# Windowed attention, second pass: where the probabilities of a group's last unit are added up

## The chip, the cores and the metric

The kernel runs on one core of one Trainium2 chip. The core has TensorE (PE in the profile, with PEld for its weight loads), VectorE (DVE), ScalarE (ACT), GpSimd (POOL) and SyncE (SP), which here only issues DMAs. The metric is the device time of one execution, in microseconds (us). Lower is better. Before the change it is 1713.32 us, the median of three runs.

## The reference, cut to what matters

The program is two transformer-like layers over 2048 tokens of width 512. The first is linear attention plus a mixture of experts, the second is windowed softmax attention plus a block over 256 chosen tokens. Everything is float32. Only the softmax attention of the second layer is touched. It has 16 heads of width 32, it is causal, and the window reaches back 1024 tokens:

```python
scores = jnp.einsum('bhqd,bhkd->bhqk', q, k) / np.sqrt(HD)
scores = jnp.where(mask[None, None, :, :], scores, NEG)   # 0 <= q_idx - k_idx <= 1024
attn = jax.nn.softmax(scores, axis=-1)
out = jnp.einsum('bhqk,bhkd->bhqd', attn, v)
out = out.transpose(0, 2, 1, 3).reshape(b, n, H)
return jnp.einsum('bnh,hm->bnm', out, w_out)
```

What the change is about is the denominator of that softmax: for each head and each query, the sum over the keys of exp(score - maximum).

## The kernel before, in words

A first pass over the scores, spread over earlier stages, finds every query's maximum. The second pass, which is the last stage of the program (from about 1342 us to the end at 1713.8 us), computes the scores again, takes the exponentials and does everything else.

The second pass goes over **groups** `(Q, g)`: Q is one of four blocks of 512 queries (four tiles of 128), g one of four sets of four heads. Their order is written out by hand in `order`: first (2,0), (0,0), (2,1), (0,1), (2,2), (0,2), (2,3), (0,3), then (1,0) to (1,3), then (3,0) to (3,3).

A group is a list of **units**, made by `units(Q)`. A unit is a block of 128 keys against the query tiles that can see it, or two blocks of keys that between them cover the four query tiles once. Blocks Q = 2 and Q = 3 have nine units, n = 0 to 8, each with all 512 queries. Q = 1 has eight units and Q = 0 has four, and there the last three are narrower: 384, 256 and 128 queries.

For one unit:

- `probabilities` has PE compute the scores into two PSUM tiles `ps` (L1296), take off the maxima (L1311) and add the masks (L1319). Then ACT takes the exponential (L1330) into two SBUF tiles of 128 keys x 2 heads x 512 queries. For n = 0 these tiles are the accumulators `acc0` and `acc1` (a pool of two per name), for the other units they are `pt` tiles (a pool of eight, so four units).
- `values` multiplies the probabilities with the values into the PSUM tile `av` (L1370).
- `gathered` adds the unit to the accumulators: `acc += pt`, two instructions of 128x1024 (L1403), on GpSimd for odd n and on VectorE for even n. For some units `summed(n)` returns True, and then `sums` is called for them instead.
- `sums` is a product of PE with a matrix of ones, `ones_f`: it sums over the 128 keys and puts the result into the PSUM tile `sm` (L1384). One such product is eight matmul instructions, two for each of the four heads. The first two heads read the first tile, the last two heads the second.

The program is software-pipelined by one unit: in the loop over the units PE first gets the scores of the next unit, then `values` and `gathered` of the unit before (`pending`).

When a group is through, its `ending` runs beside the units of the next group, one step for each unit:

```python
            for _ in range(3):
                yield
            self.sums(self.acc, 0, QT * P, True)
            for j in range(QT):
                js = slice(j * P, (j + 1) * P)
                V.reciprocal(self.sm[:, js], self.sm[:, js])
                V.tensor_tensor(aT[:, g, js], aT[:, g, js], self.sm[:, js], ALU.mult)
                if j % 2:
                    yield
```

So the product over the finished accumulators is issued with the next group's unit n = 3, just behind `values` and `gathered` of its n = 2. Four pairs of reciprocal and multiplication on VectorE follow (L1413, L1414). After the last head group, g = 3, four products with `w_out` (L1340) and four additions (L1344) give the output rows. Every engine takes its instructions in this order of the program.

Of the kernel before, what the change touches and what calls it, by code (L numbers as in the profile page):

```python
# [21 lines left out]
NT = T // P  # L22
D = 512
NC = D // P
# [14 lines left out]
def two_layer_kernel(ctx: ExitStack, tc: tile.TileContext, a: dict, out: bass.AP):  # L39
# [1227 lines left out]
    QT = 4  # L1267
# [79 lines left out]
    class Group:  # L1347
# [7 lines left out]
        def summed(self, n):  # L1355


            if (self.Q, self.g) == (NT // QT - 1, NC - 1) and n == len(self.us) - 2:
                return True
            return self.Q > 1 and n == len(self.us) - 1  # L1360

        def values(self, n, got):
            Q, g, unit = self.Q, self.g, self.us[n]
# [140 lines left out]
```

## Time and profile before

| | |
|---|---|
| median of three runs | 1713.32 us (1712.89 to 1716.47) |
| the profiled execution, its own time | 1715.47 us |
| its span, first to last instruction | 1713.8 us |
| mean granted TensorE clock | 0.994 |
| busy over the span: PE, DVE, ACT, POOL | 97%, 57%, 34%, 29% |
| busy from 1342 to 1480 us (Q = 2 and 0): PE, DVE, POOL | 137.86, 92.97, 108.28 of 138 us |
| busy from 1622 to 1695 us (most of (3,1) to (3,3)): PE, DVE, POOL | 73.00, 48.28, 58.87 of 73 us |
| products with `ones_f` (L1384) | 200 instructions, 25 products: 16 over accumulators, 9 over a single unit |

Busy time is read with care: the ends of matmuls are modelled, and a VectorE or GpSimd instruction counts as busy from its start to its end whether it works or is held up. A timeline row may merge instructions that follow one another; it then shows the form of the first, the time from the first start to the last end, and how many there are.

### The profile page before, as it was taken

Reading aid. Unit: us, or ns where it says so; the run is one execution under the profiler, and the core shown is the slowest. Engines: PE = TensorE matmul, PEld = TensorE weight load, DVE = VectorE, ACT = ScalarE, POOL = GpSimd, SP = SyncE. Lnnn points to the kernel's source line nnn. Section 1 sums busy time; section 2 is a strip of 40 time slices with the busy share of each in tenths; the row PEclk is TensorE's granted clock in tenths of the full one; section 3 lists DMA queues with packets and bytes.
Section 4 is the critical chain, followed back from the end, with each engine's and each line's share of the span. In section 5 each row is a group of like instructions: output and inputs, shape, how many; then the busy total and the mean of one; then the engine's idle time right before and its main releaser. Section 6 shows DMA issues by size and latency. Waiting matters only on the chain.

```text
span 1713.8 us, 20410 instructions
## 1 busy us (share of the span) xinstructions
PE 1657.4 (97%) x8114; PEld 743.6 (43%) x8114; DVE 982.5 (57%) x1256; ACT 588.2 (34%) x939; POOL 500.0 (29%) x398
## 2 busy tenths in 40 slices
PE   8999999999999999989999989899999999999999
PEld 3445444444444444444443434454564333333343
DVE  4754746345445543357566676675555477557565
ACT  3213333243253344221111110431100566447473
POOL 3230000000000200053574423330000677558584
PEclk9999999999999999999999999999899999999999
DMA  9411001120030431111010034112232300110101
GB/s 360 169 37 47 25 25 37 47 88 25 25 111 25 94 104 50 62 56 56 25 32 26 28 118 153 62 50 74 74 99 74 99 1 2 50 50 2 50 1 38
DMA packets 62384, 109.23 MB, mean 64 GB/s; under 512 B 12528, under 2 KB 14064, under 8 KB 61520
## 3 DMA queue, kind: packets, MB, share of 16 engines
q1 hardware_dynamic: 55856, 106.12, 18.7%
q0 software_dynamic: 1152, 1.21, 0.4%
q10 hardware_dynamic: 5280, 0.59, 0.3%
q8 instruction: 63, 1.03, 0.3%
q14 instruction: 33, 0.27, 0.1%
HBM read 86.24 MB, written 21.67 MB: 63 GB/s over the span
## 4 chain that ended last, share of the span: by engine, by line
PE 81%; DVE 10%; ACT 2%; DMA 2%; POOL 2%; issue 2%; SPq 0%; DVEq 0%; POOLq 0%; ACTq 0%
PE ea L494 6%; PE acc L478 6%; PE eg L492 6%; PE ps L1296 6%; PE pa L633 6%; PE p L965 6%; PE av L1370 5%; PE po L553 3%; PE pq L367 3%; PE po L1340 3%; PE gx L242 3%; DVE mx L645 3%; PE mg L1210 2%; PE pao L1175 2%; PE pm L1225 2%; PE po L555 2%
## 5 line engine op out<-in xcount | busy, mean ns | idle before, releaser
L645 DVE TENSOR_REDUCE mx<-pa 128x4 f32<-128x1536 f32 (+3 forms) x144 | 252.9, 1756 | 151.2 <-PE pa L641 72.2
L1403 POOL TENSOR_TENSOR acc<-acc,pt 128x1024 f32<-128x1024 f32 (+2 forms) x110 | 252.9, 2328 | 96.6 <-DVE acc L1403 43.4
L1330 ACT ACTIVATE pt<-ps 128x1024 f32<-128x1024 f32 (+3 forms) x208 | 181.4, 924 | 108.1 <-PE ps L1319 61.5
L1403 DVE TENSOR_TENSOR acc<-acc,pt 128x1024 f32<-128x1024 f32 (+1 forms) x80 | 144.4, 1832 | 103.9 <-POOL acc L1403 103.9
L633 PE MATMUL pa<-kT,qT 32*128 32x384 f32 (+3 forms) x1152 | 139.8, 541 | 19.8 <-DVE mx L645 16.1
L350 ACT ACTIVATE r_e<-eg 128x512 f32<-128x512 f32 x128 | 75.9, 594 | 201.6 <-PE eg L492 194.4
L1296 PE MATMUL ps<-qT,kT 32*128 32x512 f32 (+3 forms) x1152 | 139.9, 524 | 0.0
L352 DVE TENSOR_TENSOR h<-ea,r_e 128x512 f32<-128x512 f32 x128 | 87.2, 685 | 84.5 <-ACT r_e L351 83.5
L743 POOL TENSOR_TENSOR cosg<-cosg,gam 128x512 f32<-128x512 f32 x2 | 2.5, 1264 | 442.7 <-DVE gam L740 442.7
L492 PE MATMUL eg<-xl,rwgT 128*128 128x512 f32 x256 | 130.7, 592 | 0.0
L494 PE MATMUL ea<-xw,rw1T 128*128 128x512 f32 x256 | 130.7, 592 | 0.0
L478 PE MATMUL acc<-h,rw2T 128*128 128x512 f32 x256 | 129.2, 592 | 0.0
L965 PE MATMUL p<-w_qk,xnt 128*128 128x512 f32 x256 | 123.2, 604 | 2.3 <-DVE qk L758 2.3
L1370 PE MATMUL av<-pt,v 128*32 128x512 f32 (+3 forms) x1024 | 100.8, 482 | 0.0
L1296 PEld LDWEIGHTS ps<-qT,kT 32*128 32x128 f32 x1152 | 54.7, 183 | 94.7 <-issue 65.8
L633 PEld LDWEIGHTS pa<-kT,qT 32*128 32x128 f32 x1152 | 46.8, 185 | 103.3 <-DVE mx L645 64.9
L488 DVE TENSOR_TENSOR xw<-xw,xl 128x512 f32<-128x512 f32 x64 | 43.8, 685 | 83.5 <-DMA xw<-w_d 83.2
L351 ACT ACTIVATE r_e<-r_e 128x512 f32<-128x512 f32 x128 | 80.3, 629 | 5.7 <-ACT r_e L350 1.9
L478 PEld LDWEIGHTS acc<-h,rw2T 128*128 128x128 f32 x256 | 48.6, 190 | 61.3 <-issue 52.1
L492 PEld LDWEIGHTS eg<-xl,rwgT 128*128 128x128 f32 x256 | 48.6, 190 | 61.2 <-issue 61.0
L494 PEld LDWEIGHTS ea<-xw,rw1T 128*128 128x128 f32 x256 | 48.6, 190 | 61.2 <-issue 59.3
L288 PE MATMUL pk<-k_wT,xnT 128*128 128x512 f32 x128 | 61.3, 622 | 3.5 <-ACT xnT L117 3.5
(336 smaller groups left out, 2420.0 us busy)
## 6 DMA issues: line engine op xcount, KB each, us to landing
xw<-w_d SPq DMA_DIRECT2D x64, 256.0 KB, 3.2
x<-in_x SPq DMA_DIRECT2D x16, 256.0 KB, 4.7
res_d<-x SPq DMA_DIRECT2D x16, 256.0 KB, 2.1
xr<-res_d SPq DMA_DIRECT2D x16, 256.0 KB, 4.2
xn_d<-xn SPq DMA_DIRECT2D x16, 256.0 KB, 3.0
res_d<-xr SPq DMA_DIRECT2D x16, 256.0 KB, 3.1
xnq<-xn_d SPq DMA_DIRECT2D x16, 256.0 KB, 2.8
v_d<-vt SPq DMA_DIRECT2D x16, 256.0 KB, 2.0
```

The source lines that it names most:

```text
L351: S.activation(r, r, AF.Square)
L352: V.tensor_tensor(dst, pa, r, ALU.mult)
L478: PE.matmul(acc, rw2T[:, j, e, :], h, start=e == 0 and j == 0, stop=e == E - 1 and j == 1,)
L492: PE.matmul(pg, rwgT[:, e, hb], xl, start=True, stop=True)
L494: PE.matmul(pa, rw1T[:, e, hb], xw, start=True, stop=True)
L633: PE.matmul(pS[:, h, : w * P], qT[r, g, i * P : (i + 1) * P], kT[r, g, ks], start=True, stop=not (edge or last),)
L645: V.tensor_reduce(mx[:, g, :, c], pS[:, :, : w * P], AX.X, ALU.max)
L965: PE.matmul(pj, xnt[:, c, :], w, start=c == 0, stop=c == NC - 1)
L1296: PE.matmul(pS[h // 2][:, h % 2, t0 * P - q0 : (t1 + 1) * P - q0], kT[r, g, kb * P : (kb + 1) * P], qT[r, g, t0 * P : (t1 + 1) * P], start ...
L1330: S.activation(pT[:, :, :n], pS[hp][:, :, :n], AF.Exp)
L1370: PE.matmul(self.av[h * HD : (h + 1) * HD, t0 * P - o : (t1 + 1) * P - o], vs[kb // 4][:, kb % 4, hs], got[h // 2][:, h % 2, t0 * P - q0 : ...
L1403: eng.tensor_tensor(part, part, got[hp][:, :, : q1 - q0], ALU.add)
```

## The change

`summed` says which units are summed by a product of their own. Before, these were the last unit (n = 8) of every group with Q > 1, and also the last but one (n = 7) of the very last group (3,3). Now only the last two units of (3,3) are. The last units of (2,0) to (2,3) and (3,0) to (3,2), seven in all, are added to the accumulators by `gathered` as the others are. All have n = 8, so the code gives them to VectorE.

```diff
         def summed(self, n):
 
 
-            if (self.Q, self.g) == (NT // QT - 1, NC - 1) and n == len(self.us) - 2:
-                return True
-            return self.Q > 1 and n == len(self.us) - 1
+            return (self.Q, self.g) == (NT // QT - 1, NC - 1) and n >= len(self.us) - 2
```

In the instruction streams this takes 56 matmul instructions (7 products of 8) off PE, with their weight loads, and puts 14 additions of 128x1024 on VectorE, each pair between the pair for n = 6 and the next group's pair for n = 2. The `sm` tile of those groups is now first written by the product over the accumulators. The orders on GpSimd, ScalarE and SyncE stay as they were.

## The prediction

> **What bounds the kernel now.** I read the page first: its chain that ended last, then its costliest groups.
>
> ```profile
> span 1713.8 us, 20410 instructions
> ...
> PE 81%; DVE 10%; ACT 2%; DMA 2%; POOL 2%; issue 2%; SPq 0%; DVEq 0%; POOLq 0%; ACTq 0%
> ...
> L1403 POOL TENSOR_TENSOR acc<-acc,pt 128x1024 f32<-128x1024 f32 (+2 forms) x110 | 252.9, 2328 | 96.6 <-DVE acc L1403 43.4
> ...
> L1403 DVE TENSOR_TENSOR acc<-acc,pt 128x1024 f32<-128x1024 f32 (+1 forms) x80 | 144.4, 1832 | 103.9 <-POOL acc L1403 103.9
> ```
>
> PE carries the chain, so work off PE looks like gain. But both engines that add spend much of their time waiting for each other. So next I asked line 1403 for itself, with its min/median/max in ns, and the timelines of the two engines at the end of group (2,1):
>
> ```profile
> L1403 POOL TENSOR_TENSOR acc<-acc,pt x110: 720/2363/3406, 1342.8 to 1689.9; 128x1024 f32<-128x1024 f32 x78, 128x768 f32<-128x768 f32 x16, 128x256 f32<-128x256 f32 x16
> ...
> L1403 DVE TENSOR_TENSOR acc<-acc,pt x80: 677/1215/3386, 1345.8 to 1693.2; 128x1024 f32<-128x1024 f32 x64, 128x512 f32<-128x512 f32 x16
> ```
>
> ```profile
> 1392.22 4.50 DVE L1403 TENSOR_TENSOR acc<-acc,pt 128x1024 f32<-128x1024 f32 x2 [2.25 <-POOL acc L1403]
> ```
>
> ```profile
> 1388.78 5.72 POOL L1403 TENSOR_TENSOR acc<-acc,pt 128x1024 f32<-128x1024 f32 x2 [1.56 <-DVE acc L1403]
> ```
>
> ```profile
> 1395.72 9.11 POOL L1403 TENSOR_TENSOR acc<-acc,pt 128x1024 f32<-128x1024 f32 x4 [1.23 <-DVE acc L1403]
> ```
>
> VectorE's pair for n = 6 takes 4.50 us, though an addition of 1024 takes 1.21 alone. It starts at 1392.22, POOL's pair for n = 5 ends at 1388.78 + 5.72 = 1394.50, and VectorE ends at 1396.72: 2.22 after POOL, 1.1 for each addition. So an addition on VectorE does nothing while one on GpSimd runs. The two share something, here called the port, and the additions form one serial chain. The Trainium skill ("SBUF — State Buffer", "SBUF: two separate sides") names it: GpSimd and a VectorE instruction with two SBUF inputs exclude each other for a whole instruction. That speaks against this change; who goes next when both wait, it does not say, so by it alone the sum stays open between the first two rivals below.
>
> The last row holds four additions: n = 7 of (2,1), 5.56 us to 1401.28 (the row of a window that ends at 1400), then at once n = 1 of (0,1), narrower, 3.55 for both. Now the chain of waits at the same place:
>
> ```profile
> 1397.66 0.86 PE sm L1384 x8
> ...
> 1403.56 0.57 PE av L1370 x8
> 1404.13 0.86 PE sm L1384 x8
> 1404.98 1.07 PE ps L1296 x8
> ```
>
> One product costs PE 0.86 us. The first row is one that goes; the second is the product over the accumulators, which today finds them ready since 1401.28. Last, the tail:
>
> ```profile
> 1642.49 10.19 POOL L1403 TENSOR_TENSOR acc<-acc,pt 128x1024 f32<-128x1024 f32 x4 [1.22 <-DVE acc L1403]
> 1653.92 5.54 POOL L1403 TENSOR_TENSOR acc<-acc,pt 128x1024 f32<-128x1024 f32 x2 [1.23 <-DVE acc L1403]
> ```
>
> ```profile
> 1689.93 4.50 DVE L1403 TENSOR_TENSOR acc<-acc,pt 128x1024 f32<-128x1024 f32 x2 [2.26 <-POOL acc L1403]
> ```
>
> ```profile
> 1694.53 1.19 PE L1384 MATMUL sm<-acc,ones_f 128*32 128x512 f32 x8
> ```
>
> From n = 1 of (3,1) at 1622.54 to 1692.22 GpSimd never idles but for VectorE's turns of 1.22 to 1.56. VectorE's last pair ends at 1694.43 and the last product starts at 1694.53; the view of line 1384 puts 0.3 us of PE idle down to it. In the tail this serial chain, not PE, is already the bound, by a hair.
>
> **The change, part by part.** *Removed:* 7 products x 0.86 = 6.0 us of PE. GpSimd's and ScalarE's orders stay; `pt` buffers are held longer, at no cost: the tightest, those of n = 8 in (2,0), are wanted again by ACT at 1374.42 and will be free by 1372.4 (below).
>
> *Added:* 14 additions on VectorE, 2.22 us of port for each pair, behind GpSimd's pair for n = 7. Behind them in VectorE's queue stand the next group's n = 2 additions and the reciprocals; PE waits for them at the product over the accumulators, with all later scores behind it.
>
> *Who gets the port?* When GpSimd ends n = 7, VectorE waits for n = 8, and GpSimd has n = 1 of the next group queued (its row starts it without a gap). No L1403 row shows such a meeting. The nearest is elsewhere, in the timelines at 762 us, where both VectorE additions of steps and base read two SBUF tiles:
>
> ```profile
> 762.75 0.16 DVE L850 TENSOR_TENSOR thr_h<-steps,base_h 128x1 f32<-128x1 f32 x1
> 762.83 2.33 DVE L850 TENSOR_TENSOR thr_l<-steps,base_l 128x1 f32<-128x1 f32 x1
> ```
>
> ```profile
> 762.79 2.35 POOL L763 TENSOR_TENSOR t<-qk,cosg 128x1024 f32<-128x1024 f32 x1 [8.29 <-DVE base_h L860]
> 765.10 2.51 POOL L768 TENSOR_TENSOR t<-qk,sing 128x512 f32<-128x512 f32 x2
> ```
>
> GpSimd came between two back-to-back VectorE instructions, and thr_l then ended at 765.16, before GpSimd's next was through: they take turns, in the order in which they ask. I take **turns**: first half of n = 8, GpSimd's first half of n = 1 (3.55 / 2 = 1.78), second half of n = 8. One tiny instruction is thin evidence, so the ends stay: VectorE keeps the port for both halves, or GpSimd keeps it until its queue waits.
>
> *Groups (2,g), turns.* In (2,1) PE would come to the product at 1404.13 - 0.86 = 1403.27. The second half of n = 8 is done at 1401.28 + 1.1 + 1.78 + 1.1 = 1405.26. Then follow a handover of about 0.1 (1694.43 to 1694.53 above) and half to all of a product (0.43 to 0.86), so 0.5 to 0.95, say 0.7: PE goes on at 1405.96, not 1404.98, a loss of 1.0 net of the 0.86 gained. (2,2) and (2,3) have the same spacing. In (2,0) n = 7 ends at 1368.35 and PE goes on at 1370.55 (same views), so 1368.35 + 3.98 + 0.7 = 1373.03, a loss of 2.5. Sum 3 x 1.0 + 2.5 = +5.5 (4.6 to 6.4). Nothing later in these groups gives it back: GpSimd's n = 1 of the next one waits for PE.
>
> *Group (3,0):* GpSimd idles 11.66 us before 1622.54, so n = 8 is hidden and 0.86 is gained.
>
> *Tail:* the chain must take two more pairs, after (3,1) and (3,2): 2 x 2.22 = 4.4, or 3.9, since a GpSimd addition that had to wait is some 0.13 shorter afterwards (1401.28 - 1396.72 = 4.56 for a pair, against 4.69 for the pair at 1622.54, which did not wait) and with turns two more have to wait; I take +4.2. PE's own 2 x 0.86 there buys nothing, as PE is not last.
>
> Sum: 5.5 - 0.9 + 4.2 = **+8.8 us** (7.6 to 9.9). The profiled execution's 1715.47 (span 1713.8 and 1.67 around it) would become 1724.3; on the median of 1713.32, 2.15 lower, it is 1722.1. The measurement can tell a change of about 0.2%, 3.4 us.
>
> **The rivals.**
>
> *VectorE keeps the port.* Then n = 8 of (2,1) is done at 1401.28 + 2.22 = 1403.50 and PE goes on at 1404.2: 0.8 gained in each of three groups, 0.7 lost in (2,0), sum -1.7 (-2.0 to -0.6); with -0.9 and +4.3, +1.7 (1.0 to 2.9): 1715.0. For it: back-to-back VectorE instructions start up to 0.1 before the one ahead ends. Against it: the 762 rows.
>
> *GpSimd keeps the port.* n = 8 done at 1401.28 + 3.55 + 2.22 = 1407.05, PE at 1407.75: 2.8 lost three times and 4.3 once, 12.6. In the tail n = 8 waits for two full additions (4.65), PE stalls in (3,2) and again in (3,3), and ends some 5.2 later. Sum 12.6 - 0.9 + 5.2 = +16.9 (16 to 18): 1730.2. For it: GpSimd's rows follow each other without a gap. Against: thr_l got in.
>
> *All hidden (faster).* If a VectorE addition beside a GpSimd one took its 1.21 us, n = 8 of (2,1) would be done before 1403.27, and the chain of the tail would not grow: -6.0, 1707.3. The change decides for this side once a pair for n = 8 ends under 2.0 us after n = 7 and GpSimd's next pair is not put off. Against: 3386 ns, the longest of line 1403, and the 4.50 rows.
>
> The skill's "Perfetto Trace Analysis" ("Identifying the Most-Contended Engine") would judge by occupancy and relieve the busiest engine. By it, with PE at 97% and DVE at 57%, the change pays all that it takes off PE. The port's rows, which no occupancy shows, say otherwise and decide here.
>
> That the edit does less than it says can be excluded: the streams hold 56 matmuls fewer and 14 VectorE additions more.
>
> **How the numbers follow.** Turns 0.55, VectorE keeps 0.22, GpSimd keeps 0.13, hidden 0.10. Slower by over 0.2% are the first and third, 0.68; within 0.2% the second, 0.22; faster 0.10. The range runs from VectorE's low end, 1714.0, to 1729.5, the lower part of GpSimd's; left out are the rest of that and the hidden case. The likeliest case alone: 1720.9 to 1723.2.
>
> **What would show it.** Right: VectorE's pair for n = 8 of the (2,g) groups with an addition of GpSimd between its halves, PE idle for about 2 us for VectorE at the product over the accumulators in (2,1), 3 to 4 in (2,0), and the time from n = 1 of (3,1) to the last product longer by about 4. Wrong: n = 8 back to back (second case), or after both of GpSimd's (third), or products that wait for nothing.

## The result, and the profile after

| | before | after |
|---|---|---|
| median of five runs | 1713.32 us | 1722.46 us (1720.67 to 1722.95) |
| ratio | | 1.0049, 95% interval 1.0038 to 1.006 |
| profiled execution, span | 1715.47, 1713.8 us | 1720.67, 1719.0 us |
| first exponential of the second pass | 1337.96 us | 1334.08 us |
| from there to the end of the span | 375.81 us | 384.89 us |

The kernel became slower by 9.1 us, 0.5%. The two spans differ by 5.2 us only, because the stages ahead of the second pass, which nobody touched, took 3.9 us less in the profiled execution of after. So from here on all profiles are compared from the first exponential of the second pass (the first ScalarE row of line 1330 into `acc`) to the end. There the difference is 384.89 - 375.81 = 9.08 us, the same as that of the medians.

The page of after: the chain that ended last, and the two groups of additions, now line 1401.

```profile
span 1719.0 us, 20334 instructions
...
PE 75%; DVE 12%; POOL 4%; issue 3%; DMA 3%; ACT 3%; SPq 0%; DVEq 0%; POOLq 0%; ACTq 0%
...
L1401 POOL TENSOR_TENSOR acc<-acc,pt 128x1024 f32<-128x1024 f32 (+2 forms) x110 | 264.3, 2431 | 94.5 <-DVE acc L1401 40.9
L1401 DVE TENSOR_TENSOR acc<-acc,pt 128x1024 f32<-128x1024 f32 (+1 forms) x94 | 184.1, 1993 | 78.5 <-POOL acc L1401 76.5
```

PE has 56 matmuls less, and its share of the chain has fallen from 81% to 75%: the chain now runs through VectorE, GpSimd and "issue" instead. GpSimd has the same 110 additions as before, but they take 11.4 us longer: an addition that is held up counts as busy. Who waits for them is said by the view of the product's line (now 1382), before a row of 0.3 us, once:

```profile
  DVE acc L1401: 21.8, 16
```

This row adds the idle time of PE's weight loads to that of its matmuls, and the two overlap. The view of line 1401 has them apart; the matmuls alone wait six times, for 6.8 us:

```profile
  PEld sm L1382: 15.0, 10
  PE sm L1382: 6.8, 6
```

The timelines of VectorE and GpSimd at the end of (2,1), each for a window that ends before the next pair, and the chain of waits at the same place:

```profile
1397.68 6.12 DVE L1401 TENSOR_TENSOR acc<-acc,pt 128x1024 f32<-128x1024 f32 x2 [2.26 <-POOL acc L1401]
```

```profile
1397.60 5.12 POOL L1401 TENSOR_TENSOR acc<-acc,pt 128x1024 f32<-128x1024 f32 x2
```

```profile
1399.83 0.02 issue
1399.85 0.02 ACT pt L1330
1399.88 0.47 issue
1400.35 0.60 ACT pt L1330
1400.95 0.02 issue
1400.97 2.85 DVE acc L1401
1403.81 0.04 issue
1403.86 1.05 PE sm L1382 x4
1404.91 1.07 PE ps L1296 x8
```

VectorE's pair for n = 8 takes 6.12 us. The GpSimd row holds the second half of n = 7 (2.36 us, to 1399.96) and the first half of (0,1)'s n = 1, which ends at 1402.72. VectorE's first half ends at 1401.04, its second at 1403.80. So after n = 7 the order is VectorE, GpSimd, VectorE: turns, one addition each. PE's timeline shows what it does meanwhile:

```profile
1401.92 1.03 PE L1382 MATMUL sm<-acc,ones_f 128*32 128x512 f32 x4
1403.86 1.05 PE L1382 MATMUL sm<-acc,ones_f 128*32 128x512 f32 x4 [0.91 <-DVE acc L1401]
1404.84 1.14 PE L1296 MATMUL ps<-qT,kT 32*128 32x512 f32 x8
```

The first half of the product, four matmuls over the first accumulator, runs ahead. Then PE has no work that it may do for 0.91 us, until VectorE's second half is through. The other half of the product takes 1.05 us in the chain before the next scores.

The tail, on GpSimd's timeline, where the rows of four additions hold n = 7 of one group and n = 1 of the next:

```profile
1624.10 4.68 POOL L1401 TENSOR_TENSOR acc<-acc,pt 128x1024 f32<-128x1024 f32 x2 [10.95 <-PE av L1368]
...
1644.04 12.13 POOL L1401 TENSOR_TENSOR acc<-acc,pt 128x1024 f32<-128x1024 f32 x4 [1.23 <-ACT pt L1330]
...
1671.43 12.12 POOL L1401 TENSOR_TENSOR acc<-acc,pt 128x1024 f32<-128x1024 f32 x4 [1.23 <-ACT acc L1330]
```

The first of these rows of four took 10.19 us before and takes 12.13, the second 10.21 and 12.12: VectorE's two halves of n = 8 are inside them. The product over the accumulators of (3,2) now waits as well, as PE's timeline says:

```profile
1681.40 1.05 PE L1382 MATMUL sm<-acc,ones_f 128*32 128x512 f32 x4 [1.97 <-DVE acc L1401]
```

### The profile page after: what moved, and what is told of

It is laid out like the page before. It is cut to its first block, busy times and chain, and to the rows that moved or that the text cites. A ratio compares the mean times of both kernels' runs of the same rounds, so it can differ in the third digit from the quotient of the medians.

```text
span 1719.0 us, 20334 instructions
## 1 busy us (share of the span) xinstructions
PE 1657.5 (96%) x8058; PEld 742.3 (43%) x8058; DVE 1021.7 (59%) x1270; ACT 588.2 (34%) x939; POOL 511.5 (30%) x398
## 3 DMA queue, kind: packets, MB, share of 16 engines
q0 software_dynamic: 1152, 1.21, 0.4%
## 4 chain that ended last, share of the span: by engine, by line
PE 75%; DVE 12%; POOL 4%; issue 3%; DMA 3%; ACT 3%; SPq 0%; DVEq 0%; POOLq 0%; ACTq 0%
PE eg L492 6%; PE acc L478 6%; PE ea L494 6%; PE pa L633 6%; PE p L965 5%; PE ps L1296 4%; PE av L1368 4%; PE po L553 3%; PE pq L367 3%; PE po L1340 3%; PE gx L242 3%; DVE acc L1401 2%; DVE mx L645 2%; POOL acc L1401 2%; PE mg L1210 2%
## 5 line engine op out<-in xcount | busy, mean ns | idle before, releaser
L1401 POOL TENSOR_TENSOR acc<-acc,pt 128x1024 f32<-128x1024 f32 (+2 forms) x110 | 264.3, 2431 | 94.5 <-DVE acc L1401 40.9
L1401 DVE TENSOR_TENSOR acc<-acc,pt 128x1024 f32<-128x1024 f32 (+1 forms) x94 | 184.1, 1993 | 78.5 <-POOL acc L1401 76.5
L763 POOL TENSOR_TENSOR t<-qk,cosg 128x1024 f32<-128x1024 f32 x15 | 35.3, 2351 | 98.7 <-DVE qk L758 63.1
```

What stands on the lines that cost most here:

```text
L1401: eng.tensor_tensor(part, part, got[hp][:, :, : q1 - q0], ALU.add)
```

## Experiments

The theory tested is that of the prediction: an addition on VectorE and one on GpSimd exclude each other and take turns, which costs PE a wait in the groups of block 2 and lengthens a serial chain at the end. Its first rival is that VectorE simply has too much to do, the second that the whole loss lies in the tail. Ratios are to the kernel before on the same chip; the last column is the profile's, from the first exponential of the second pass to the end, against 375.81 us.

| kernel | median us | ratio, 95% interval | profile, us |
|---|---|---|---|
| changed kernel | 1722.46 | 1.0049 (1.0038 to 1.006) | +9.1 |
| change for block 2 alone | 1721.66 | 1.0042 (1.0028 to 1.0056) | +6.4 |
| change for block 3 alone | 1717.64 | 1.0019 (1.001 to 1.0028) | +2.9 |
| change for (3,0) alone | 1713.86 | 1.0 (0.9991 to 1.0009) | -0.8 |
| change, n = 8 on GpSimd | 1732.68 | 1.0113 (1.0098 to 1.0128) | +19.7 |
| change, n = 1 on VectorE too | 1706.66 | 0.9953 (0.994 to 0.9967) | -7.5 |
| products kept, n = 1 on VectorE | 1710.79 | 0.9986 (0.9977 to 0.9995) | -2.3 |
| change, all additions on VectorE | 1707.05 | 0.9962 (0.9948 to 0.9975) | -7.5 |
| change, GpSimd n = 1 and 5 | 1732.84 | 1.0117 (1.0101 to 1.0132) | +18.9 |
| products kept, GpSimd n = 1 and 5 | 1722.79 | 1.0052 (1.0038 to 1.0066) | +10.1 |
| change, GpSimd n = 3 | 1705.7 | 0.9961 (0.9947 to 0.9974) | -7.6 |

**Where it falls.** Three kernels do one part of the change each.

```diff
-            return self.Q > 1 and n == len(self.us) - 1
+            return self.Q == 3 and n == len(self.us) - 1                                        # block 2 changed
+            return (self.Q == 2 or (self.Q, self.g) == (3, NC - 1)) and n == len(self.us) - 1   # block 3 changed
+            return self.Q > 1 and (self.Q, self.g) != (3, 0) and n == len(self.us) - 1          # (3,0) changed
```

> The change for block Q = 2 alone: (2,0) to (2,3) add n = 8 on VectorE, block 3 keeps its products. Theory 'turns' (the additions of VectorE and GpSimd exclude each other and take turns, PE waits for the second half of n = 8): from one group's first exponential to the next the pairs (2,g),(0,g) are longer by 2.6 us for g = 0 and 1.2 for each of the others, 6.2 in all, and the tail from (3,1) on is as before: +6.2 us, about 1719.5. Rival 'VectorE is full' (what costs is VectorE's own added time, wherever it falls): 8 of 14 additions, so 8/14 of 9.1 us, +5.2, and not in these places alone. Rival 'the tail did it' (the serial chain at the end carries the whole loss): faster by 4 x 0.86 = 3.4, about 1710.

> The change for block Q = 3 alone: (3,0), (3,1) and (3,2) add n = 8 on VectorE, block 2 keeps its products. 'Turns': 0.86 us gained once by (3,0), 2 x 0.86 gained on PE but 4.2 us more in the serial chain at the end: +2.9 us measured from the first exponential of (3,1) to the end, about 1716.2. 'VectorE is full': 6 of 14 additions, +3.9. 'The tail did it': +9.1 + 3.4 = +12.5.

> The change for group (3,0) alone, where GpSimd has some 11 us of idle time behind n = 7. 'Turns': n = 8 meets no addition of GpSimd, each half takes 1.2 us, no product waits, and the 0.86 us of the removed product are gained, shifting all of the tail: 1712.5, -0.05%, at the limit of what can be told; by the profile the stretch from the first exponential of (3,1) to that of (3,2) is 24.3 to 24.4 us, not 25.2. 'VectorE is full': +1.3 (2 of 14 additions).

The parts are 6.4 and 2.9 us, 9.3 together for 9.1 of the whole. In the first kernel the stretches from the first exponential of (0,g) to that of the next group are longer by 2.8 us for g = 0 and by 1.22 for each of the other three (9.94 before, 12.72 and 11.16), and everything behind is as before. This refutes the rival of the tail, and VectorE's added time is not what sets it, since the same two additions cost 2.8, 1.2 or, in (3,0), nothing. The third kernel shows that last case; by its time alone it can't be told from before. Its VectorE timeline has the pair for n = 8 of (3,0), with GpSimd idle:

```profile
1611.42 2.36 DVE L1403 TENSOR_TENSOR acc<-acc,pt 128x1024 f32<-128x1024 f32 x2 [2.05 <-ACT pt L1330]
```

2.36 us for the pair, not 6.12, and the stretch from (3,1) to (3,2) is 24.38 us instead of 25.18: the 0.8 us of the removed product.

**The other engine.** The additions of n = 8 can also be given to GpSimd, with `eng = G if n % 2 or n == 8 else V`.

> The changed kernel with n = 8 added by GpSimd, right behind its n = 7, instead of by VectorE. 'Turns' (one serial chain, whichever engine works): n = 8 is done 4.7 us after n = 7, PE goes on 0.7 later: 1.7 us lost in (2,1) to (2,3) each, 3.2 in (2,0), 0.9 gained at (3,0), and two more GpSimd pairs in the tail's chain, 9.2: +16.6, about 1730. 'VectorE is full': VectorE has no more work than before, so it is as fast as before or 6 us faster.

It is slower still, by 19.7 us in the profile, somewhat more than expected. Block 3 gave the 8.3 us expected, block 2 11.1 instead of 8.3. VectorE has no more to do than before, so its load is not the cause.

**No meeting at n = 8.** Then the place of the meeting is taken away, by giving n = 1 to VectorE:

```diff
-                eng = G if n % 2 else V
+                eng = G if n % 2 and n > 1 else V
```

> The changed kernel, and besides the additions of n = 1 of every group are done by VectorE too, so GpSimd has only n = 3, 5 and 7 and nothing queued when it ends n = 7. 'Turns': VectorE's two halves of n = 8 follow each other, done 2.2 us behind GpSimd's n = 7; a group's serial chain is 3 x 4.6 + 5 x 2.2 = 24.8 us, not 27.2, against 24.3 of PE, so most of the loss goes: (2,1) to (2,3) gain some 0.8 each, (2,0) loses 0.7, the tail loses up to 1.5: about 1711 to 1714. 'VectorE is full': 32 more additions on VectorE, more than twice the 14 of the change, so it is slower than the changed kernel: 1735 or more.

It beats both kernels, by more than expected. VectorE has 126 additions instead of 94 and still no product waits for one: the view of line 1382 has no row for an addition any more. At the end of (2,1) VectorE's timeline has one row for n = 8 and for n = 1 and the first half of n = 2 of (0,1):

```profile
1395.58 6.85 DVE L1401 TENSOR_TENSOR acc<-acc,pt 128x1024 f32<-128x1024 f32 x5 [2.25 <-POOL acc L1401]
```

Five additions in 6.85 us, where the changed kernel had two in 6.12. I had expected that the loss would stay in (2,0) and in the tail. I had shortened the chain behind n = 7 and not ahead of it: with n = 1 on VectorE, n = 7 itself is done sooner. Counted from the first exponential of the next group, GpSimd ends it after 3.5 us in (2,1), where the changed kernel needs 4.7, and after 3.2 in (2,0), where it needs 6.1. In (2,1) that is at 1397.87, and the product starts at 1401.17.

The same division without the change tells what the change is then worth:

> The kernel of before, its products kept, with the additions of n = 1 of every group on VectorE: what this division is worth without the change. 'Turns': in the kernel of before the additions held PE up by 0.3 us at the end and by 1.4 to 1.7 us at block 1's outputs, so about 1.9 us faster than before, 1711 to 1712; the changed kernel with this division lies 6.0 below it less what still waits, so 5 to 6. If instead the division alone made all of that kernel's gain and the products cost nothing, this one is as fast as it, 1706 to 1707.

The division alone gives 2.3 us, 1.6 of them in (3,0), where block 1's outputs stand; the change on top of it gives 373.55 - 368.29 = 5.3 us, 0.75 to 0.8 for each of the seven products (9.94 to 9.19 us in block 2, 25.12 to 24.33 in block 3). So the product that is removed has a value. What the change paid was the meeting of the additions.

**One engine.** With `eng = V` no two additions can meet at all.

> The changed kernel with every addition on VectorE, none on GpSimd: no two additions can meet. 'Turns': each addition takes 1.21 us and none 3.4; VectorE has 16 x 1.2 + 5.3 of reciprocals and multiplications = 24.6 us for a group of nine units against 24.3 of PE, so it is nearly bound by VectorE and close to the quarter division: 1706 to 1711. 'VectorE is full': the slowest of all, over 1750.

As expected. The view of line 1401 has min/median/max, in ns, of all 204 additions on VectorE:

```profile
L1401 DVE TENSOR_TENSOR acc<-acc,pt x204: 418/1218/1227, 1338.3 to 1679.4; 128x1024 f32<-128x1024 f32 x78, 128x768 f32<-128x768 f32 x8, 128x512 f32<-128x512 f32 x8, 128x256 f32<-128x256 f32 x8
```

None is longer than 1.23 us, where the changed kernel's longest is 3.39. The shapes at the end of such a row are counted on a sample of its instructions. Twice the additions on VectorE, and the kernel is faster: the rival of the full VectorE is refuted.

**A division that failed.** Another division, n = 1 and n = 5 on GpSimd, was run with the change and without it: `eng = G if n % 4 == 1 else V`.

> The changed kernel with GpSimd adding only units n = 1 and n = 5, VectorE all others. 'Turns': a group's serial chain is 2 x 4.6 + 6 x 2.2 = 22.4 us, under PE's 24.3, so the additions are hidden again and the 7 products removed are gained whole: 7 x 0.86 = 6.0, and up to 1 more from the tail's end and the outputs of block 1, which stand behind additions in VectorE's queue: 1706 to 1707.5. 'VectorE is full': far more additions on VectorE, slower than the changed kernel, over 1735.

> The kernel of before (last units summed by products) with GpSimd adding only units n = 1 and n = 5. It tells what the division of the additions is worth without the change. 'Turns': in the kernel of before the chain held PE up by 0.3 us at the end and by about 1.4 us where block 1's outputs wait, so 0.3 to 1.7 gained: 1711.6 to 1713. The changed kernel with the same division should then lie 6.0 below it. 'VectorE is full': slower than before by 5 or more.

Both expectations failed by far, the changed kernel's by 25 us, and the kernel with products is slower than before as well. The timelines of (2,2) in the former show a break in the chain, first on VectorE, then on GpSimd:

```profile
1409.57 6.77 DVE L1401 TENSOR_TENSOR acc<-acc,pt 128x1024 f32<-128x1024 f32 x4 [1.67 <-POOL acc L1401]
1416.27 0.95 DVE L1411 RECIPROCAL sm<-sm 128x128 f32<-128x128 f32 x1
...
1420.10 1.22 DVE L1401 TENSOR_TENSOR acc<-acc,pt 128x1024 f32<-128x1024 f32 x1
```

```profile
1407.18 4.68 POOL L1401 TENSOR_TENSOR acc<-acc,pt 128x1024 f32<-128x1024 f32 x2 [7.40 <-PE av L1368]
1421.47 2.37 POOL L1401 TENSOR_TENSOR acc<-acc,pt 128x1024 f32<-128x1024 f32 x1 [9.61 <-DVE acc L1401]
```

VectorE adds n = 2 and 3, and then its queue holds reciprocals and multiplications until 1420.10. Only then comes n = 4, for which n = 5 waits: GpSimd sits idle for 9.61 us. I had summed the additions as if the chain ran without a break; the reciprocals on VectorE are in the chain as soon as the unit beside them is not GpSimd's. In the kernel before and in the changed one, GpSimd adds n = 3 just then.

What the break costs depends on what follows it. In block 2 of the changed kernel with this division, (2,0) alone has no reciprocals beside its units, as no group is ahead of it. The stretch behind it, from the first exponential of (0,0) to the next group's, is 0.75 us shorter than before; behind each of the other three it is 2.3 us longer. VectorE's rows for (2,0) and for n = 8 of (2,2):

```profile
1352.59 9.05 DVE L1401 TENSOR_TENSOR acc<-acc,pt 128x1024 f32<-128x1024 f32 x6 [2.24 <-POOL acc L1401]
```

```profile
1431.91 5.59 DVE L1401 TENSOR_TENSOR acc<-acc,pt 128x1024 f32<-128x1024 f32 x2
```

In (2,0) the six additions of n = 6, 7 and 8 follow each other without a break. In (2,2) n = 8 comes late, meets n = 1 of (0,2) again, and its pair takes 5.59 us. With the products kept nothing is added at n = 8, and block 2 loses nothing (-0.2 us), although GpSimd is idle for the same 9.61 us there. Of that kernel's 10.1 us, 7.9 lie in block 1, which the change does not touch: there and right behind it PE waits 2.3 us for the addition of an output row, and three times 1.4 to 1.8 us for the accumulators.

To test that the place beside the reciprocals is what counts, the last kernel gives GpSimd that unit alone: `eng = G if n == 3 else V`.

> The changed kernel with GpSimd adding n = 3 alone, VectorE all others. 'Turns', corrected by the runs with n = 1 and 5 on GpSimd (what counts is not the sum of the additions alone, but that GpSimd adds while VectorE is at the four reciprocals, which stand between its n = 2 and n = 4): n = 3 is added beside the reciprocals, the serial chain is 4.6 + 7 x 2.2 = 20 us, VectorE's own work 7 x 2.4 + 5.3 = 22.1, both under PE's 24.3; no product waits and it is as fast as with n = 3, 5 and 7 on GpSimd or better: 1705 to 1707. If any division that leaves GpSimd one or two units lost by that alone, it would be 1720 or more, like n = 1 and 5.

As expected: 7.6 us faster than before in the profile, no product waits for an addition. It, n = 1 on VectorE and all on VectorE can't be told apart by their intervals, and each beats both kernels. What counts is where the units lie, not how many of them GpSimd has.

## Why the prediction was right

It took turns as the likeliest case and 1722.1 us; the median is 1722.46, in the range, and slower by more than can be mistaken. By its steps:

| step | predicted us | measured us |
|---|---|---|
| (2,0): wait less product | +2.5 | +2.6 |
| (2,1) to (2,3), each | +1.0 | +1.2 |
| block 2, sum | +5.5 (4.6 to 6.4) | +6.2 |
| (3,0) | -0.9 | -0.8 |
| tail | +4.2 (3.9 to 4.4) | +3.7 |
| sum | +8.8 | +9.1 |

The measured figures of block 2 are the stretches from the first exponential of (0,g) to that of the next group, 9.94 us before against 12.53 and three times 11.14 after (2.59 + 3 x 1.20 = 6.2). The tail is the rest from (3,1) on, 2.9 us, without the 0.8 that (3,0) gave.

- *Who gets the port.* The step that could go three ways rested on one meeting, that of a VectorE instruction on a 128x1 tile at 762 us, so that it came out right is in part luck. All six groups in which n = 8 meets GpSimd show the same order, VectorE, GpSimd, VectorE. The rivals in which one engine keeps the port did not occur, and with them their 1715.0 and 1730.2. The rule of the Trainium skill ("SBUF — State Buffer", "SBUF: two separate sides"), that one of the two fully blocks for a whole instruction, agrees with 3.37 us for an addition of 1.21 and with the kernel in which none meets another. The order of turns, on which the sum hung, is the runs' alone.
- *PE's wait.* Mis-sized a little: 0.5 to 0.95 us, taken as 0.7, from the end of VectorE's second half to PE's next scores. The chain has 1404.91 - 1403.80 = 1.1. The step that was short is the half product: taken as 0.43 to 0.86, it measures 1.05. The 0.86 is the piece of a chain without a break, counted from the end of the matmuls ahead; behind a wait there is nothing ahead that it could overlap. The second halves in turn came slightly sooner (1403.80 - 1399.96 = 3.84 against 3.98).
- *PE's idle time.* The forecast was about 2 us in (2,1) and 3 to 4 in (2,0), where its own sum gives 2.7. PE's weight loads idled that long (1.8 us in (2,1), 0.9 + 2.6 in (2,0)). Its matmuls, which are the work, idled 0.91 us in (2,1) and 0.40 + 1.69 in (2,0), since half of the product runs while VectorE's second half is outstanding.
- *The removed product.* 0.86 in the chain, 0.75 to 0.80 where it was removed with nothing waiting.
- *The tail.* 3.7 and not 4.2: a pair for n = 8 adds 1.9 to the rows of four, the lower of the two bounds, as the additions of GpSimd that had to wait are shorter afterwards. So block 2 was forecast 0.7 too low and the tail 0.5 too high; that the sum is off by 0.3 only is luck.
- *The range.* Its lower end, 1714.0, is 0.3 below the sum of the case that it is taken from (1713.32 + 1.0). The measured time is far from both ends.
- *All hidden.* That case was rightly put last for this kernel, yet its number, 1707.3, is what the kernels reach in which n = 8 meets no addition of n = 1 on GpSimd (1705.7 to 1707.05). In them, part of the gain is the division's own 2.3 us.

The advice by occupancy failed here in the way that the prediction said: VectorE at 57% had room, but its additions had no room beside GpSimd's. But the section that the prediction cites for it (the Trainium skill, "Perfetto Trace Analysis", "Identifying the Most-Contended Engine") does not take the busy share of matmuls as TensorE's measure, so the 97% is not its number. And work taken off PE did pay, 5.3 us, once the additions were divided otherwise.

## What to carry to other kernels

Before moving work from PE to a vector engine, look at the min, median and max of the same instruction there: a maximum of nearly three times the median, beside work of the other vector engine, is a sign that the two exclude each other. If the timelines bear it out, their times must be added as one chain. Price the new work at the place where it meets the other engine, in the unit in which someone waits for it; the same pair of additions cost 2.6, 1.2 and 0 us in three places. And before dividing such a chain anew, go through the queue of each engine in order: what else stands in it, like the reciprocals here, is part of the chain where the other engine has nothing to do beside it.

## What the hardware showed that was not expected

Half a product takes PE as long as a whole one. Before the change, PE's timeline at the product over the accumulators of (2,1) has all eight matmuls:

```profile
1403.94 1.04 PE L1384 MATMUL sm<-acc,ones_f 128*32 128x512 f32 x8
1404.92 1.14 PE L1296 MATMUL ps<-qT,kT 32*128 32x512 f32 x8
```

After it, the four matmuls of the last two heads, with the other two heads already done, take 1.05 us, and the next scores start 0.98 us behind the first matmul in both kernels (1404.92 - 1403.94 and 1404.84 - 1403.86). One such matmul takes 0.592 us by the view of its line, and eight of them 1.04, so the heads run beside each other, and leaving two of them out shortens nothing. It was only seen where a wait splits the product.
